# Four graph layers on one core: one-hots by place in the block, and sums joined on VectorE

## The chip, the cores and the metric

The kernel runs on one core of a Trainium2 chip. The metric is the device time in microseconds (us). Over three runs the median is 5306.94 us (5293.82 to 5309.91). One further execution was taken with the hardware profiler, and every line of profile in this document comes from such an execution.

## The reference

There are 6250 nodes with 256 features, and 100000 directed edges, sorted by their destination `dst`. Four layers of message passing follow each other. Each takes the normalised, rectified features, passes messages along the edges, sums them at the destination, and adds the result to `x`:

```python
h = jnp.maximum(_layernorm(x), 0.0); x = x + layer(h, ...)      # four times

# layer 0: attention with 8 heads, logits from per-node scores s, self loops
alpha = leaky_relu(s[src] + s[dst], 0.2)
e = exp(alpha - segment_max(alpha, dst)[dst])
attn = segment_sum(Vh[src] * (e / segment_sum(e, dst)[dst])[:, :, None], dst)
h = batch_norm(x + attn @ Wo + bo); h = batch_norm(h + relu(h @ W1 + b1) @ W2 + b2)
# layer 1: messages times a filter made from 32 edge features and a cutoff
agg = segment_sum(hl[src] * (rbf @ W_r2m.T + b_r2m) * C[:, None], dst)
# layer 2: attention with one head, logits from the gathered row and 128 edge features
out = relu(segment_sum(xj * softmax_by_dst(a)[..., None], dst))
# layer 3: graph convolution with self loops
out = relu(segment_sum(xw[src] * (dinv[src] * dinv[dst])[:, None], dst) + b)
```

Everything is fp32. What matters here is `segment_sum`: sums of edge rows, by destination, once in every layer (256 to 265 columns, 128 in layer 1).

## The kernel before, in words

The nodes are padded to 6272 and lie in 49 blocks of 128, node n on partition n mod 128. The edges lie in 98 groups of 1024, each as 128 partitions by 8 columns. As the edges are sorted, the destinations of group g fall into a window of 128 nodes that starts at node 64g − 32 (checked at run time; a slower path exists for other data and isn't taken here). `rel` holds each edge's destination relative to its window.

A stage of edges is a loop over the groups. For a group, GpSimd issues eight indirect DMAs (`gather`, L130), each of which fetches 128 source rows from a table in DRAM; they go into a ring of tiles, several groups ahead. VectorE makes eight one-hots of 128x128 (`rel` compared with `iota`, in layers 1 and 2 also multiplied by a weight). TensorE multiplies one-hots and rows in eight matmuls that add up in one PSUM tile S, two in turn (`sum_window`, L666 to L673; the eight matmuls are L670). In fp32 a matmul leaves two records in the trace. So S holds the sums of the window's nodes, with the window's first node on partition 0.

A window starts at partition 96 or 32 of a block, so the sums lie 32 or 96 partitions off. In layers 0, 2 and 3 ScalarE therefore copies S to SBUF (`ws`, L672; in layer 3 L1158), and `sum_block` (L675 to L681) builds block b's sum in a PSUM tile T out of up to four windows, each multiplied by a shifted identity (`shifts`, four matmuls at L680, on every second group). `blocks_done` tells after which group a block is whole.

The stages, in the order of the program, by the span of the profile:

- Rows of layer 0 (0 to 180 us): per block layernorm, transposes, the value row and the score terms, written to table `vt`. Between the blocks the list `checks` is worked off on VectorE, one entry after every fourth block; it fills `rel` too.
- e0 (180 to about 1430 us): layer 0's edges. `scw` holds the nodes' score terms laid out by window (four tiles made by shift matmuls at L706 to L712, copied at L714), and `place`, from GpSimd's iota at L716, the node number at each partition of a window. For group g: `logits0` (L746 to L756) uses the gathered rows and the destination's terms, which `of_dst` (L743) fetches with a transposed one-hot from L729; L816 multiplies the rows with the exponentials; L670 sums. On odd groups `attn0` (L758 to L766) finishes a block, `turn0` (L772 to L774) transposes it, and one group later `project0` (L780) and `residual0` (L788, L790) multiply it with the output weights. At groups 6 and 8, `made` prepares weights of layers 1 and 2 on TensorE and VectorE through PSUM tag B.
- Feed-forward and batch norms of layer 0, and the table for layer 1 (1432 to about 1867 us).
- e1 (gathers from 1700 to 2915 us): layer 1 sums with swapped operands (L1008), so that nodes lie along the columns: `agg`, with a column for each node. VectorE adds the columns that the last window has already begun (64 at L1035), ScalarE copies the others (64 at L1036). L994 multiplies a finished block, L1026 makes layer 2's table row.
- e2 (3017 to 4132 us, finished at 4177): layer 2, with `one_hot2` (L1075, logits and weight on VectorE and ScalarE), `sum_window`, `sum_block`, `out2`, and the table row for layer 3.
- e3 (4177 to 5292 us, finished at 5321): layer 3, with `one_hot3` (L1130), the sum at L1154, the copy at L1158, `sum_block`, and `end3` (L1134 to L1141), which adds the node's own row from `rows3`, scales, adds the bias, rectifies and writes out.

The order inside e0 to e3 is written by hand (`manual_schedule`): each engine works its instructions in the order of the program, and only semaphores between engines delay them. GpSimd's queue holds the gathers and little else; SP's queue holds the loads and stores of rows. [...]

Of the kernel before, what the change touches and what calls it, by code (L numbers as in the profile page):

```python
# [35 lines left out]
def tile_gnn(ctx: ExitStack, tc: tile.TileContext, a: dict, out: bass.AP, N: int):  # L36

# [70 lines left out]
    shifts = const.tile([P, 3 * P], F32, name="shifts")  # L108
    nc.gpsimd.memset(shifts, 0.0)
    make_identity(nc, shifts[:, P:2 * P])  # L110
# [78 lines left out]
    with ExitStack() as l0:  # L189
# [52 lines left out]
        def row0(b):  # L242
# [3 lines left out]
            for k in range(2):  # L246
# [13 lines left out]

        rel3 = rel.rearrange("p (g j) -> p g j", j=J)
# [5 lines left out]
                  lambda: nc.vector.tensor_scalar(bad[:, 1:2], bad[:, 1:2], P - 1.0, None, OP.subtract)]  # L267
# [377 lines left out]
    def fast():  # L645
        wp = fctx.enter_context(tc.tile_pool(name="wl", bufs=1))
        psc = fctx.enter_context(ExitStack())
        ps = psc.enter_context(Psum("ps0", S=2, A=2, T=1, B=2, E=1))

        def one_hot(pool, g):  # L650

            oh = pool.tile([P, J, P], F32, name="oh")
            nc.vector.tensor_tensor(oh, iota[:, None, :].to_broadcast([P, J, P]),
                                    rel[:, g * J:(g + 1) * J][:, :, None].to_broadcast([P, J, P]),
                                    OP.is_equal)
            return oh

        def shift_by(s):

            return shifts[:, P - s:2 * P - s]  # L660

        def windows_of(b):

            return [(g, HW * g - OFF - P * b) for g in range(max(0, 2 * b - 1), min(G, 2 * b + 3))]

        def sum_window(pool, oh, rows, n):  # L666

            s = ps("S", [P, n])
            for j in range(J):
                nc.tensor.matmul(s, oh[:, j, :], rows[:, j, :], start=j == 0, stop=j == J - 1)  # L670
            ws = pool.tile([P, n], F32, name="ws", bufs=6)
            nc.scalar.activation(ws, s, AF.Copy)  # L672
            return ws  # L673

        def sum_block(sums, b, n):  # L675

            t = ps("T", [P, n])
            parts = windows_of(b)
            for i, (g, s) in enumerate(parts):
                nc.tensor.matmul(t, shift_by(s), sums[g], start=i == 0, stop=i == len(parts) - 1)  # L680
            return t  # L681
# [16 lines left out]
        with tc.tile_pool(name="e0", bufs=2) as ep:  # L698

            scw = ep.tile([P, NB, 2, 2 * H], F32, name="scw", bufs=1)  # L700
            for odd in range(2):
                for b0, b1 in ((0, 32), (32, NB)):
                    t = ps("AB"[odd], [P, b1 - b0, 2 * H])
                    if odd:
                        b2 = min(b1, NB - 1)
                        nc.tensor.matmul(t, shift_by(-OFF), sc[:, b0:b1, :], start=True, stop=False)  # L706
                        nc.tensor.matmul(t[:, 0:b2 - b0, :], shift_by(P - OFF), sc[:, b0 + 1:b2 + 1, :],
                                         start=False, stop=True)
                    else:
                        b2 = max(b0, 1)  # L710
                        nc.tensor.matmul(t, shift_by(OFF), sc[:, b0:b1, :], start=True, stop=False)
                        nc.tensor.matmul(t[:, b2 - b0:, :], shift_by(OFF - P), sc[:, b2 - 1:b1 - 1, :],  # L712
                                         start=False, stop=True)
                    nc.vector.tensor_copy(scw[:, b0:b1, odd, :], t)  # L714
            place = ep.tile([P, G], F32, name="place", bufs=1)
            nc.gpsimd.iota(place, pattern=[[HW, G]], base=-OFF, channel_multiplier=1,  # L716
                           allow_small_or_imprecise_dtypes=True)
            sums, drows, tos, dgs, ohs, vs, ms, mts = {}, {}, {}, {}, {}, {}, {}, {}
# [73 lines left out]
            with tc.manual_schedule():  # L792
# [5 lines left out]
                for g in range(G + 2):  # L798
# [11 lines left out]
                    summed = [(b, sum_block(sums, b, VR)) for b in blocks_done(g - 1)]  # L810
# [8 lines left out]
                    for b, s in summed:  # L819
                        attn0(b, s)  # L820
                    if g < G:
                        sums[g] = sum_window(ep, ohs[g], vg, VR)
                    for b, s in summed:
                        turn0(b)
# [106 lines left out]
        with tc.tile_pool(name="e1", bufs=2) as ep, Psum("ps1", S=2, A=3, B=1, C=1, K=1) as ps:  # L931
# [7 lines left out]
            agg = ep.tile([P, HW * (G - 1) + P], F32, name="agg", bufs=1)  # L939
# [38 lines left out]
            with tc.manual_schedule():  # L978
# [6 lines left out]
                for g in range(G + 2):  # L985
# [6 lines left out]
                    for b in blocks_done(g - 1):  # L992
                        t = ps("B", [P, D])
                        nc.tensor.matmul(t, agg[:, OFF + b * P:OFF + (b + 1) * P], w1["out"],  # L994
# [36 lines left out]
                    if g < G:  # L1031
                        old = HW if g else 0
                        c = HW * g
                        if old:
                            nc.vector.tensor_tensor(agg[:, c:c + old], agg[:, c:c + old], s[:, 0:old], OP.add)  # L1035
                        nc.scalar.activation(agg[:, c + old:c + P], s[:, old:P], AF.Copy)  # L1036
# [9 lines left out]
        with tc.tile_pool(name="e2", bufs=2) as ep:  # L1046
            vgs, sums, normed = {}, {}, {}
# [60 lines left out]
            with tc.manual_schedule():  # L1108
                for g in range(G + 2):
                    if ahead <= g < G:  # L1110
                        rows2(g)
                    summed = [(b, sum_block(sums, b, TR)) for b in blocks_done(g - 1)]
# [3 lines left out]
                    for b, s in summed:  # L1116
                        normed[b] = out2(b, s)
                    if g < G:
                        sums[g] = sum_window(ep, oh, vgs[g], TR)
# [384 lines left out]
```

## Time and profile before

| what | value |
|---|---|
| median of three runs | 5306.94 us |
| profiled execution | 5323.26 us |
| its span | 5321.5 us |
| mean granted clock of TensorE | 0.746 |
| busy: TensorE, VectorE, ScalarE, GpSimd | 3068.8, 2089.9, 609.6, 3036.3 us |
| moved by DMA | 536.81 MB, 101 GB/s |

The span is the time from the first to the last instruction of the profiled execution. Busy times are sums over the span; an engine that waits or only issues is not busy. The granted clock says how fast TensorE was allowed to run, 1 being full speed. An idle time is put down to the event that ended it: the name of an instruction on another engine, "issue" where nothing visible held the engine, and "remote" where the event could not be traced to an instruction. PEld is TensorE's loading of weights, which overlaps with its matmuls.

### The profile page before, as it was taken

Reading aid. Unit: us, or ns where it says so; the run is one execution under the profiler, and the core shown is the slowest. Engines: PE = TensorE matmul, PEld = TensorE weight load, DVE = VectorE, ACT = ScalarE, POOL = GpSimd, SP = SyncE. Lnnn points to the kernel's source line nnn. Section 1 sums busy time; section 2 is a strip of 40 time slices with the busy share of each in tenths; the row PEclk is TensorE's granted clock in tenths of the full one; section 3 lists DMA queues with packets and bytes.
Section 4 is the critical chain, followed back from the end, with each engine's and each line's share of the span. In section 5 each row is a group of like instructions: output and inputs, shape, how many; then the busy total and the mean of one; then the engine's idle time right before and its main releaser. Section 6 shows DMA issues by size and latency. Waiting matters only on the chain.

```text
span 5321.5 us, 42644 instructions
## 1 busy us (share of the span) xinstructions
PE 3068.8 (58%) x12132; PEld 2383.4 (45%) x12133; DVE 2089.9 (39%) x6391; ACT 609.6 (11%) x1559; POOL 3036.3 (57%) x3215
## 2 busy tenths in 40 slices
PE   7577777787896144444444545555555345554545
PEld 4366666666645133333333434444444333443334
DVE  5355555555525155555555623333333112221222
ACT  3100000000134000000000012222222100000000
POOL 0456666666203655656555266666666566666665
PEclk9777777777897567777777777777777677776777
DMA  2444444444301233333333233333333233333332
GB/s 96 124 127 139 137 141 139 139 138 136 110 0 56 60 95 100 98 103 102 97 96 103 74 96 99 97 98 100 100 99 97 76 93 99 97 97 97 98 97 84
DMA packets 258746, 536.81 MB, mean 101 GB/s; under 512 B 65096, under 2 KB 144966, under 8 KB 258502
## 3 DMA queue, kind: packets, MB, share of 16 engines
q0 software_dynamic: 137984, 364.28, 25.3%
q1 hardware_dynamic: 107750, 156.85, 9.2%
q10 hardware_dynamic: 12768, 12.85, 0.8%
q8 instruction: 103, 1.69, 0.1%
q14 instruction: 141, 1.16, 0.1%
HBM read 504.57 MB, written 29.15 MB: 100 GB/s over the span
## 4 chain that ended last, share of the span: by engine, by line
PE 35%; another core or an unknown queue 23%; issue 18%; DVE 8%; POOL 8%; ACT 5%; DMA 2%; ACTq 0%; DVEq 0%; SPq 0%; POOLq 0%
PE ps_S L670 13%; PE ps_S L1154 5%; POOL vg L130 5%; PE ps_A L743 3%; POOL big L130 3%; PE ps_T L680 3%; DVE oh L968 2%; PE ps_A L441 2%; PE ps_B L447 2%; PE ps_Q L245 1%; DVE big L1005 1%; PE ps_S L1008 1%; PE ps_B L780 1%; ACT L1072 1%
## 5 line engine op out<-in xcount | busy, mean ns | idle before, releaser
L130 POOL DMA_INDIRECT vg<-xt,src_i x1568 | 1488.6, 949 | 888.7 <-issue 543.1
L130 POOL DMA_INDIRECT big<-ht,src_i x784 | 740.4, 944 | 482.8 <-PE ps_S L1008 185.2
L130 POOL DMA_INDIRECT xbuf<-vt,src_i x784 | 764.5, 975 | 437.2 <-PE ps_S L670 191.3
L670 PE MATMUL ps_S<-vg,oh 128*128 128x258 f32 x1568 | 473.1, 467 | 435.4 <-DVE oh L1075 422.5
L680 PE MATMUL ps_T<-ws,shifts 128*128 128x265 f32 (+2 forms) x1164 | 342.4, 435 | 479.7 <-issue 319.6
L670 PEld LDWEIGHTS ps_S<-vg,oh 128*128 128x128 f32 x1568 | 371.7, 241 | 523.5 <-DVE oh L1075 436.8
L1154 PE MATMUL ps_S<-vg,oh 128*128 128x256 f32 x1568 | 431.8, 428 | 162.7 <-issue 129.3
L670 PE MATMUL ps_S<-xbuf,oh 128*128 128x265 f32 x1568 | 497.6, 480 | 20.2 <-issue 18.2
L680 PEld LDWEIGHTS ps_T<-ws,shifts 128*128 128x128 f32 x1164 | 243.0, 214 | 559.5 <-issue 397.5
L1075 DVE TENSOR_SCALAR oh<-iota,rel,ex 128x128 f32<-128x128 f32 x784 | 210.4, 359 | 662.8 <-ACT ex L1072 510.1
L1154 PEld LDWEIGHTS ps_S<-vg,oh 128*128 128x128 f32 x1568 | 342.8, 219 | 238.2 <-issue 177.1
L670 PEld LDWEIGHTS ps_S<-xbuf,oh 128*128 128x128 f32 x1568 | 371.3, 243 | 109.6 <-issue 24.8
L1130 DVE TENSOR_SCALAR oh<-iota,rel 128x128 f32<-128x128 f32 x784 | 163.1, 296 | 579.8 <-remote 413.1
L1008 PE MATMUL ps_S<-oh,big 128*128 128x128 f32 x1568 | 287.2, 357 | 172.2 <-issue 138.0
L1008 PEld LDWEIGHTS ps_S<-oh,big 128*128 128x128 f32 x1568 | 276.6, 268 | 196.8 <-issue 149.7
L994 PE MATMUL ps_B<-wout,agg 128*128 128x256 f32 x98 | 55.9, 671 | 535.0 <-DVE agg L1035 368.1
L816 DVE TENSOR_TENSOR xbuf<-xbuf,ps_E 128x2048 f32<-128x2048 f32 x98 | 223.8, 2283 | 320.6 <-issue 145.0
L743 PEld LDWEIGHTS ps_A<-scw,to 128*128 128x128 f32 x1568 | 248.7, 246 | 61.9 <-DVE to L729 45.8
L743 PE MATMUL ps_A<-scw,to 128*128 128x16 f32 x1568 | 243.8, 301 | 52.0 <-DVE to L729 48.6
L994 PEld LDWEIGHTS ps_B<-wout,agg 128*128 128x128 f32 x98 | 23.6, 299 | 553.4 <-issue 330.8
L672 ACT ACTIVATE ws<-ps_S 128x265 f32<-128x265 f32 (+1 forms) x196 | 76.3, 389 | 1702.0 <-PE ps_S L670 803.1
L960 PE MATMUL ps_A<-wr,rb 99*128 99x384 f32 (+1 forms) x588 | 207.7, 493 | 9.3 <-issue 9.3
(228 smaller groups left out, 3419.5 us busy)
## 6 DMA issues: line engine op xcount, KB each, us to landing
drow<-in_dst_row SPq DMA_DIRECT2D x98, 512.0 KB
ea<-in_edge_attr SPq DMA_DIRECT2D x98, 512.0 KB
vg<-xt,src_i POOLq DMA_INDIRECT x1568
xbuf<-vt,src_i POOLq DMA_INDIRECT x784
big<-ht,src_i POOLq DMA_INDIRECT x784
rb<-in_rbf SPq DMA_DIRECT2D x196, 49.5 KB
vt<-row SPq DMA_DIRECT2D x49, 132.5 KB
xt<-row SPq DMA_DIRECT2D x49, 129.0 KB
```

What stands on the lines that cost most here:

```text
L130: nc.gpsimd.indirect_dma_start(out=rows, out_offset=None, in_=table, in_offset=bass.IndirectOffsetOnAxis(ap=idx[:, j:j + 1], axis=0))
L441: nc.tensor.matmul(t[:, :n], w["w1"][:, k, m * P:(m + 1) * P], hn[:, k, :n], start=k == 0, stop=k == 1)
L447: nc.tensor.matmul(t[:, :n], w["w2"][:, m, o * P:(o + 1) * P], f[:, m, :n], start=m == 0, stop=m == 3)
L670: nc.tensor.matmul(s, oh[:, j, :], rows[:, j, :], start=j == 0, stop=j == J - 1)
L680: nc.tensor.matmul(t, shift_by(s), sums[g], start=i == 0, stop=i == len(parts) - 1)
L743: nc.tensor.matmul(dgs[g][:, j, :], tos[g][:, j * P:(j + 1) * P], scw[:, g // 2, g % 2, :], start=True, stop=True)
L816: nc.vector.tensor_tensor(vals, vals, ex[:, :, :, None].to_broadcast([P, J, H, HD]), OP.mult)
L960: nc.tensor.matmul(t, rbs[g][0:33 * n, g % 2, q, :], wr3[0:33 * n, 0:n, :], start=True, stop=True)
L1008: nc.tensor.matmul(s, hg[:, j, :], ohs[g][:, j, :], start=j == 0, stop=j == J - 1)
L1075: nc.vector.tensor_scalar(oh[:, j, :], iota, rel[:, g * J + j:g * J + j + 1], ex[:, j:j + 1], OP.is_equal, OP.mult)
L1130: nc.vector.tensor_scalar(oh[:, j, :], iota, rel[:, g * J + j:g * J + j + 1], None, OP.is_equal)
L1154: nc.tensor.matmul(s, oh[:, J - 1 - j, :], vg[:, J - 1 - j, :], start=j == 0, stop=j == J - 1)
```

## The change: what it does

`rel` becomes the destination's place in its block, `dst & 127`, so that a sum lies on its own node's partition from the start. A window covers four quarters of 32 partitions, of two blocks; the shift matmuls and their constant go. Instead, `join` adds quarters of the last group's copy (`ws`) and of this group's PSUM sum on VectorE, into a PSUM tile T: two adds of 32 partitions per group, in e0 and e2. ScalarE's copy of S stays there. In layer 3 there is no copy: `add3` adds the PSUM sum into `rows3` directly, in two or three parts, and `end3` starts from there, with the bias in a PSUM tile. In layer 1 `agg` loses its offset, so that the additions and copies of 64 columns fall into pieces of 32 and 64. `scw` and `place` are made by copies on ScalarE and VectorE. T gets two PSUM banks, and B one. In e0, `join` stands behind the multiplication of the rows and ahead of `attn0`; in e2, behind the one-hots and ahead of `out2`; in e3, `add3` stands behind the next group's one-hots.

```diff
+                  lambda: nc.vector.tensor_single_scalar(rel.bitcast(I32), dst_i, P - 1, op=OP.bitwise_and),
+                  lambda: nc.vector.tensor_copy(rel, rel.bitcast(I32))]
...
-        ps = psc.enter_context(Psum("ps0", S=2, A=2, T=1, B=2, E=1))
+        ps = psc.enter_context(Psum("ps0", S=2, A=2, T=2, B=1, E=1))
...
-        def sum_block(sums, b, n):
-
-            t = ps("T", [P, n])
-            parts = windows_of(b)
-            for i, (g, s) in enumerate(parts):
-                nc.tensor.matmul(t, shift_by(s), sums[g], start=i == 0, stop=i == len(parts) - 1)
-            return t
+        def join(g, blocks, s, ws, n):
+
+
+            b = g // 2
+            quarters = [(b, 1), (b, 2)] if g % 2 else [(b - 1, 3), (b, 0)]
+            if g == G - 1:
+                quarters.append((b, 3))
+            for c, q in quarters:
+                if c < 0:
+                    continue
+                if c not in blocks:
+                    blocks[c] = ps("T", [P, n])
+                r = slice(q * Q, (q + 1) * Q)
+                if g == 0 or (g == G - 1 and q == 3):
+                    nc.vector.tensor_copy(blocks[c][r, :], s[r, :])
+                else:
+                    nc.vector.tensor_tensor(blocks[c][r, :], ws[r, :], s[r, :], OP.add)
...
+            nc.scalar.activation(scw[:, :, 0, :], sc, AF.Copy)
+            nc.vector.tensor_copy(scw[:, :, 1, :], sc)
+            nc.scalar.activation(scw[L, 1:NB, 0, :], sc[L, 0:NB - 1, :], AF.Copy)
+            nc.vector.tensor_copy(scw[F, 0:NB - 1, 1, :], sc[F, 1:NB, :])
...
-            nc.gpsimd.iota(place, pattern=[[HW, G]], base=-OFF, channel_multiplier=1,
-                           allow_small_or_imprecise_dtypes=True)
+            nc.vector.tensor_copy(place, nodeid[:, :, None].to_broadcast([P, NB, 2]))
...
-                    summed = [(b, sum_block(sums, b, VR)) for b in blocks_done(g - 1)]
...
-                    for b, s in summed:
-                        attn0(b, s)
+                    if 0 < g <= G:
+                        join(g - 1, totals, sums[g - 1], kepts.get(g - 2), VR)
+                    for b in blocks_done(g - 1):
+                        attn0(b, totals[b])
                     if g < G:
-                        sums[g] = sum_window(ep, ohs[g], vg, VR)
+                        sums[g] = sum_window(ohs[g], vg, VR)
+                        kepts[g] = kept(ep, sums[g], VR)
...
-                        if old:
-                            nc.vector.tensor_tensor(agg[:, c:c + old], agg[:, c:c + old], s[:, 0:old], OP.add)
-                        nc.scalar.activation(agg[:, c + old:c + P], s[:, old:P], AF.Copy)
+                        c = g // 2 * P
+                        if g == 0:
+                            old, new = [], [(0, 3 * Q)]
+                        elif g % 2 == 0:
+                            old, new = [(c - Q, c), (c, c + Q)], [(c + Q, c + 3 * Q)]
+                        else:
+                            old, new = [(c + Q, c + 3 * Q)], [(c + 3 * Q, c + P), (c + P, c + P + Q)]
...
+            def add3(g, s):
+                b = g // 2
+                parts = [(b, Q, 2 * Q), (b, 2 * Q, P), (b + 1, 0, Q)] if g % 2 else [(b - 1, 3 * Q, P), (b, 0, 3 * Q)]
+                for c, r0, r1 in parts:
+                    if 0 <= c < NB:
+                        nc.vector.tensor_tensor(rows3[r0:r1, c, :], rows3[r0:r1, c, :], s[r0:r1, :], OP.add)
+
+            def end3(b):
                 r0, r1 = b * P, min(N, (b + 1) * P)
-                nc.vector.tensor_tensor(s, s, rows3[:, b, :], OP.add)
-                nc.vector.scalar_tensor_tensor(s, s, dinv[:, b:b + 1], brow, op0=OP.mult, op1=OP.add)
+                t = ps("T", [P, D])
+                nc.vector.scalar_tensor_tensor(t, rows3[:, b, :], dinv[:, b:b + 1], bias, op0=OP.mult, op1=OP.add)
...
-                    sums[g] = ep.tile([P, D], F32, name="ws", bufs=6)
-                    nc.scalar.activation(sums[g], s, AF.Copy)
-                for b, s in summed:
-                    end3(b, s)
+                    sums[g] = s
+                if g > 0:
+                    add3(g - 1, sums[g - 1])
+                for b in blocks_done(g - 1):
+                    end3(b)
```

## The prediction

> **What bounds the kernel now.** I began with the slices of the page: TensorE, VectorE and GpSimd are all 40 to 60% busy, so nothing is full. The costliest groups come next (form, count | busy, mean ns | idle time before, and what ended it):
>
> ```profile
> L130 POOL DMA_INDIRECT vg<-xt,src_i x1568 | 1488.6, 949 | 888.7 <-issue 543.1
> ...
> L680 PE MATMUL ps_T<-ws,shifts 128*128 128x265 f32 (+2 forms) x1164 | 342.4, 435 | 479.7 <-issue 319.6
> ...
> L1154 PE MATMUL ps_S<-vg,oh 128*128 128x256 f32 x1568 | 431.8, 428 | 162.7 <-issue 129.3
> ```
>
> The shift matmuls that go away (L680) hold TensorE for 342 us. What they are worth depends on what each stage waits for, so the busy time by stage is next (columns: stretch, length, then busy time and count of PE, PE's weight loads, VectorE, ScalarE, GpSimd, then granted clock, DMA share, GB/s). The four rows are the edge stages of layers 0 to 3, called e0 to e3:
>
> ```profile
> 180.00:1379.00 1199.00, 878.04 (x3845) 735.74 (x3844) 603.47 (x1654) 88.63 (x327) 763.81 (x785) 0.76 0.48 140
> ...
> 1700.00:2915.00 1215.00, 520.22 (x2248) 412.65 (x2249) 585.96 (x1466) 51.59 (x211) 739.23 (x783) 0.69 0.35 96
> 3017.00:4132.00 1115.00, 588.59 (x2145) 471.19 (x2145) 333.75 (x1369) 235.95 (x461) 742.18 (x783) 0.73 0.36 98
> ...
> 4177.00:5292.00 1115.00, 542.95 (x1882) 422.53 (x1883) 214.03 (x882) 34.89 (x93) 743.91 (x783) 0.71 0.34 98
> ```
>
> e2 and e3 do different work and take the same 1115 us for the same 784 gathers: 1115/784 = 1.42 us per gather. The timeline of GpSimd in both shows how:
>
> ```profile
> 3405.21 0.94 POOL L130 DMA_INDIRECT vg<-xt,src_i  x1 [3.07 <-remote]
> 3406.46 0.95 POOL L130 DMA_INDIRECT vg<-xt,src_i  x1 [0.30 <-issue]
> ...
> 3427.99 0.95 POOL L130 DMA_INDIRECT vg<-xt,src_i  x1 [3.08 <-remote]
> ...
> 4576.28 0.94 POOL L130 DMA_INDIRECT vg<-xt,src_i  x1 [5.38 <-remote]
> ...
> 4622.18 0.94 POOL L130 DMA_INDIRECT vg<-xt,src_i  x1 [5.97 <-remote]
> ```
>
> Gathers issue 1.25 us apart, then pause until something "remote". e2 does 16 per 22.78 us (3405.21 to 3427.99), e3 32 per 45.90 us: 1.42 and 1.43 us per gather, though the rounds differ twofold. I read this as a service behind the gathers of 1.42 us each, with GpSimd running ahead of it. While it has a backlog the other engines learn of finished matmuls late; that is what the longest waits show:
>
> ```profile
> ACT ws L672 <- remote: 742.7, 77, 32.5
> ACT ws L1158 <- remote: 623.4, 31, 35.3
> ...
> DVE oh L1130 <- remote: 413.1, 30, 34.0
> ...
> DVE m L761 <- PE ps_S L670: 71.7, 12, 7.7
> ```
>
> (total us, times, longest.) Waits of 35 us for a copy of a sum long computed are not TensorE's doing. So e2 and e3 are bound by gathers. e0's 784 gathers at the same 1.42 would take 1115 of its 1199 us: 84 us in which the service lies idle, all that e0 can give back. e1 (narrower rows) goes by pairs of groups of some 25 us.
>
> **The change, part by part.** Sums are made against the profiled execution, 5323.3 us (span 5321.5 and 1.8 around it). It lies 16.3 above the median of the runs shown, 5306.9, and that difference is taken off at the end. A measurement of this kernel can tell about 0.3%, 16 us.
>
> Node stage: two more passes over the 128x784 destinations, about 1 us each on VectorE by the row of its 128x1024 compare (0.75 us), while POOL and SP are busy there; cost 0 to 2, taken 1. The eight shift matmuls and four copies of the window scores become copies on ScalarE and VectorE: the copies showed 0.44 to 0.69 us each, beside TensorE's node work. The place table leaves GpSimd's queue, where it began at 220.59 behind the first gathers; L729 waited 10.8 us for it. Group 0's chain starts earlier, but the gathers ran meanwhile; only the stall of some 5 us that follows, when the ring of rows is full, comes back: −5 (0 to −10).
>
> e0, steady. Per pair of groups, TensorE loses four shift matmuls and VectorE gains four adds of 32 partitions. Here is one odd group in the timeline:
>
> ```profile
> 627.78 1.95 PE L680 MATMUL ps_T<-ws,shifts 128*128 128x265 f32 x8
> ...
> 630.15 2.28 DVE L816 TENSOR_TENSOR xbuf<-xbuf,ps_E 128x2048 f32<-128x2048 f32 x1
> ...
> 630.38 1.93 PE L743 MATMUL ps_A<-scw,to 128*128 128x16 f32 x16 [0.65 <-DVE to L729]
> 632.35 0.41 DVE L761 TENSOR_TENSOR m<-v,ps_T 128x256 f32<-128x256 f32 x1
> 632.53 5.39 PE L670 MATMUL ps_S<-xbuf,oh 128*128 128x265 f32 x16 [0.22 <-issue]
> ```
>
> The 1.95 us of L680 end at 629.7, before L743 has its one-hot (630.2), and L670 waits for L816's end (632.4): here the removal saves nothing. Elsewhere L680 waits for the copy ws and L743 is queued behind it. To place the 84 idle us I let every gather of the timeline take 1.42 us after its issue, one behind the other, and looked where that runs dry: about 24 lie before 363 us (start, and the preparation of layer 1's weights at group 6); the other 60 are 0.5 to 0.8 per pair and eight stalls of some 4.6 where an odd group's sum comes too late to be seen before the backlog. How many go I can't read off; bounds: 0 and −60 from idle time, against +60 if more pairs miss. I take half of the gain, −30.
>
> The adds: the row of a 128x256 add is 0.41 us, step 0.46; a lane works on as many elements when 32 lanes run, so 4 x 0.46 = 1.85 us per pair. They lie behind L816, ahead of L761 and of the next one-hots L735; the sum L670 waits for neither, and in steady state VectorE idles half the time (603 of 1199), which hides them. Where the cover is gone, in the drain after the last gather, a pair takes 14.45 us and is VectorE's: 1.85 x 2.5 pairs = +4.5. **A rule against the change**: the Trainium skill, "VectorE: DVE Perf Modes", § Two Vector instructions with no wait between them, says that an instruction which starts in another group of 32 partitions than the last is held until all earlier ones have finished. The rows show the overlap it would lose: L761 started 0.08 us before L816's end. Six held instructions a pair would be 0.5 us, 1.2 more in the drain and 24 over e0's 49 pairs if uncovered. By the row it is 4.5, by the rule 5.7; I keep 4.5.
>
> PSUM goes from T=1, B=2 to T=2, B=1: the two weight preparations (groups 6 and 8) ping-pong between TensorE and VectorE through B; +3.5 (0 to 7). The transposes of L772 and the projection L780 share the one B too, but lie a group apart.
>
> e1: the offset layout makes an even group two adds of 32 columns where there was one of 64. The 128x8 operation L763 takes 0.17 and a 128x64 0.21; a step of 0.15 on the path after the sum, 49 times, is +7.4; the third copy per pair is ScalarE's (52 of 1215 us busy), nothing; the drain adds 0.6. Sum +8.
>
> e2: 0 while the gathers bound it, hidden under 1.42 x 16 = 22.8 us a round against 16.1 that a pair takes unhindered in the drain; after the last gather the join (2 x 0.46) stands ahead of the output chain, +2. e3: a copy, shift matmuls and one add become adds straight into the kept rows. The sum's PSUM buffer is now freed by VectorE behind its one-hots (8 x 0.21), 2.6 us after the sum is seen, while TensorE still has about 4 us of the next sum: 0. At the end two shift groups (1.89 and 1.46) and their copies go, two pairs of adds come: −3.5.
>
> Sum: 1 − 5 − 30 + 4.5 + 3.5 + 8 + 2 − 3.5 = −19.5. 5323.3 − 19.5 − 16.3 = **5287 us**, 0.4% below the median.
>
> **Rivals.** *Gathers everywhere* (0.15): e0 keeps its idle time too, the removed matmuls lay beside it. Then +10.5 on the same sum, 5317; 5291 to 5323 covers it. For it: the odd group above. Against it: 72 us in which L761 waited for TensorE's sums.
>
> *Slower: more late sums in e0* (0.32). Place: odd groups. The group restarts at 628.0 and its sum ends at 637.9, about 10 us later, when finished matmuls begin to be seen late; so the pair sits on the edge. Without the 1.95 us of shift matmuls TensorE idles ahead of L743 and may run slower: L743 is 1.93 us here and 3.43 at half clock, and "TensorE: Matmul & The Clock Gate", § Part 1, says that an idle window of about 3.4 us takes the clock to half. The row bears it out: this stretch had 0.86 granted, and after ten nearly idle microseconds 0.52. A half-clock sum adds 1.5 us or more, and each miss 4.6. By the row's present misses (8 of 49) nothing changes; by the rule a miss in every second pair is 16 x 4.6 = +74, without the gain of 30: 5391; in every pair 41 x 4.6 = +189, 5506. It decides from about the fifteenth miss (half of the gain eaten, and the 10.5 more).
>
> *A large gain* (0.11): the pauses in e2 and e3 belong to TensorE's events, not to a service. Then fewer matmuls let gathers run at 1.25: 0.17 x 784 x 2 = −267, 5020; or e0 loses its 60 whole: 5257. Against the first: the same 1.42 in rounds of two lengths.
>
> **How the numbers follow.** Forecast 0.42, from 5250 to 5300 and nearly all of it faster by more than 16. With 0.10 of the large gain faster is 0.52; same is 0.16 (the rival of gathers and the forecast's edge), slower 0.32. For 8 in 10, the low end takes in most of e0's idle time and some of the hidden stalls, 5215, the high end the slower case with a miss in every second pair, 5390.
>
> **What would show it.** Right: no L680, some 196 joins in e0 and as many in e2, each near 0.4 us, e2 and e3 at 1115 ± 3 us from first to last gather, e0's gathers in about 1165, e1 longer by some 7. Wrong: e0 at 1199 or above with GpSimd's gaps at even groups (late sums), a granted clock below 0.70 in e0, or rounds in e2 and e3 other than 22.8 and 45.9 us: then the service was not what bounds them.

## The result

The changed kernel takes 5382.7 us (median of four runs, 5368.3 to 5411.6) beside 5308.4 for the kernel before: a ratio of 1.0146, 95% interval 1.0113 to 1.0179. It is slower. The forecast was 5287 and faster; the time lies inside the range, on the side of the rival "more late sums in e0".

One thing has to be said ahead of all comparisons: the same kernel before took about 5310 us in some batches of runs, 5253 in others and 4498 in the rest. Each run below is therefore set beside the runs of the kernel before that were made in turn with it on the same chip, and that time is named ("beside 5318").

The profiled execution of the changed kernel took 5382.1 us (span 5380.3) against 5323.3. Its busy time over the four edge stages, from first to last gather (columns as in the table by stage of before):

```profile
182.00:1400.00 1218.00, 783.14 (x3460) 663.42 (x3461) 684.70 (x1832) 89.27 (x329) 768.24 (x784) 0.74 0.47 137
1727.00:2984.00 1257.00, 523.17 (x2251) 413.54 (x2252) 589.74 (x1510) 54.24 (x254) 745.14 (x784) 0.69 0.33 92
3085.00:4193.00 1108.00, 518.91 (x1780) 396.51 (x1779) 416.50 (x1556) 236.10 (x461) 746.60 (x784) 0.72 0.37 99
4241.00:5350.00 1109.00, 445.38 (x1504) 359.40 (x1504) 288.42 (x1055) 0.00 (x0) 747.27 (x784) 0.69 0.34 98
```

TensorE lost 95 us of work in e0, 70 in e2 and 98 in e3, and VectorE gained 81, 83 and 74. The time does not follow these amounts. By the first and last gather of each stage, the span's 58.8 us are: e0 +18.8, the stretch from e0's last gather to e1's first +7.3, e1 **+40.4**, e2 −8.7, e3 −7.5, and 8.5 in the rest (1.6 before e0, 0.1 between e1 and e2, 4.1 between e2 and e3, 2.7 at the end). The joins cost what was expected (operation, count, minimum, median and maximum in ns):

```profile
L682 DVE TENSOR_TENSOR ps_T<-ws,ps_S x388: 419/435/455, 263.4 to 4230.2; 32x265 f32<-32x265 f32 x97, 32x258 f32<-32x258 f32 x97
```

In e1 the picture changed more than its work. In GpSimd's timeline before, a round of 16 gathers stops after twelve, goes on, and the next round starts 6.38 us after the sixteenth:

```profile
2394.26 0.94 POOL L130 DMA_INDIRECT big<-ht,src_i  x1 [3.71 <-PE ps_S L1008]
...
2408.05 0.95 POOL L130 DMA_INDIRECT big<-ht,src_i  x1 [0.31 <-issue]
2410.32 0.94 POOL L130 DMA_INDIRECT big<-ht,src_i  x1 [1.31 <-remote]
...
2414.06 0.94 POOL L130 DMA_INDIRECT big<-ht,src_i  x1 [0.30 <-issue]
2420.44 0.94 POOL L130 DMA_INDIRECT big<-ht,src_i  x1 [5.43 <-PE ps_S L1008]
```

After, all sixteen go out without a stop, and the next round starts 8.47 us after the last:

```profile
2421.83 0.95 POOL L128 DMA_INDIRECT big<-ht,src_i  x1 [7.55 <-PE ps_S L1008]
...
2440.68 0.95 POOL L128 DMA_INDIRECT big<-ht,src_i  x1 [0.30 <-issue]
2449.15 0.95 POOL L128 DMA_INDIRECT big<-ht,src_i  x1 [7.53 <-PE ps_S L1008]
```

What the round waits for is the chain that begins with the table row's add on VectorE (the add in the round before, then the chain after):

```profile
2415.80 0.43 DVE L1026 TENSOR_TENSOR row<-ps_C,bn 128x258 f32<-128x258 f32 x1 [11.82 <-remote]
```

```profile
2444.54 0.43 DVE L1026 TENSOR_TENSOR row<-ps_C,bn 128x258 f32<-128x258 f32 x1 [13.20 <-remote]
2444.89 2.13 DVE L968 TENSOR_SCALAR oh<-iota,rel,cut 128x128 f32<-128x128 f32 x8
2446.94 0.28 DVE L1041 TENSOR_TENSOR agg<-agg,ps_S 128x32 f32<-128x32 f32 x2
2447.13 1.34 DVE L1005 TENSOR_TENSOR big<-big,ps_A 128x384 f32<-128x384 f32 x3
```

From L1026 to the gathers' restart it is 4.61 us here and 4.64 before (2415.80 to 2420.44): the extra piece of 32 columns costs nothing visible. But L1026 itself is released later. If each gather takes 1.42 us from its issue, one behind the other, these sixteen are worked off at 2444.55, and L1026 starts at 2444.54. Before, they were worked off at 2416.98 and L1026 started 1.18 us ahead of that. This pair of rounds is a clear case and not the typical one: over the 49 rounds L1026 starts at the median 1.3 us ahead before and 0.7 us ahead after. By the same reckoning the service idles 105 us in all of e1 before and 145 after, which is e1's whole growth.

### The profile page after: what moved, and what is told of

Its sections match the earlier page's. It is cut to its first block, busy times and chain, and to the rows that moved or that the text cites. A ratio compares the mean times of both kernels' runs of the same rounds, so it can differ in the third digit from the quotient of the medians.

```text
span 5380.3 us, 40826 instructions
## 1 busy us (share of the span) xinstructions
PE 2802.3 (52%) x10952; PEld 2166.3 (40%) x10953; DVE 2351.2 (44%) x7031; ACT 577.2 (11%) x1511; POOL 3050.5 (57%) x3211
## 4 chain that ended last, share of the span: by engine, by line
another core or an unknown queue 26%; PE 19%; DVE 13%; issue 7%; ACT 4%; POOL 2%; DMA 0%; DVEq 0%; ACTq 0%; POOLq 0%
PE ps_S L1174 8%; PE ps_S L655 5%; DVE oh L968 3%; DVE big L1005 2%; DVE oh L1084 2%; DVE ea L1010 2%; DVE te L1011 2%; PE ps_A L442 2%; PE ps_B L448 2%; POOL big L128 1%; POOL vg L128 1%; ACT L1081 1%; ACT L124 1%; PE ps_S L1008 1%
## 5 line engine op out<-in xcount | busy, mean ns | idle before, releaser
L1174 PE MATMUL ps_S<-vg,oh 128*128 128x256 f32 x1568 | 461.3, 465 | 674.7 <-issue 598.3
L1174 PEld LDWEIGHTS ps_S<-vg,oh 128*128 128x128 f32 x1568 | 372.7, 242 | 763.6 <-issue 659.4
L655 PEld LDWEIGHTS ps_S<-vg,oh 128*128 128x128 f32 x1568 | 368.6, 241 | 606.9 <-DVE oh L1084 489.8
L1026 DVE TENSOR_TENSOR row<-ps_C,bn 128x258 f32<-128x258 f32 x49 | 20.9, 427 | 497.3 <-remote 468.7
L968 DVE TENSOR_SCALAR oh<-iota,rel,cut 128x128 f32<-128x128 f32 x784 | 209.4, 349 | 0.0
```

Of the source, the lines that this page charges most:

```text
L968: nc.vector.tensor_scalar(ohs[g][:, j, :], iota, rel[:, c], w1["cut"][:, c], OP.is_equal, OP.mult)
L1174: nc.tensor.matmul(s, oh[:, J - 1 - j, :], vg[:, J - 1 - j, :], start=j == 0, stop=j == J - 1)
```

## Experiments

### The parts alone

The changed kernel's e0 in the kernel before (four small operations ahead of layer 1 turn `rel` back from places in the block to places in the window):

```diff
 # e0, row stage, scw, place and PSUM shares of the changed kernel; layers 1 to 3 of the kernel before
+        turn_rel(False)      # rel = rel - start + 128 * (rel < start), start 96 or 32
```

> The changed kernel's e0 alone (with its row stage, scw, place, joins, PSUM shares), and the kernel before in layers 1, 2 and 3; between them four small VectorE operations turn the places in the block back into places in the window, some 2 us. Theory E0, that the loss on the slower chips lies in e0 (joins and the single B bank, more late sums): on a chip where the kernel before takes 5250 to 5310, +30 to +75 us; on one where it takes 4498, within 8 us. Rival E1, that the loss lies in layer 1's pieces of 32 columns: within 20 us of before on either.

Measured: 5361.1 us beside 5318.1, ratio 1.0112 (1.0065 to 1.0160).

The changed kernel's layer 1 in the kernel before:

```diff
+        turn_rel(True)
 # e1 of the changed kernel: agg without offset, pieces of 32 and 64 columns
+        turn_rel(False)
```

> The kernel before with the changed kernel's layer 1 alone (agg without offset, pieces of 32 and 64 columns), and eight small VectorE operations around it that turn the places, some 4 us. The split of the add alone did not lengthen e1 on a slower chip (1168 against 1216), so theory E0 says: within 20 us of before on a slower chip, within 8 on a faster one. Rival E1: +25 to +45 on a slower chip.

Measured: 5344.3 beside 5318.1, ratio 1.0050 (1.0033 to 1.0067). And the whole, beside both:

> The changed kernel as a whole on the same chip as the two parts. On a slower chip +50 to +90 us over the kernel before, as in the first result, on a faster one within 5. If the parts add up, this is new_e0 plus new_e1 plus what layers 2 and 3 give; by theory E0 nearly all of it is new_e0's.

Measured: 5379.6, ratio 1.0153 (1.0089 to 1.0217). So the loss repeats, and within the intervals its parts add up: 1.12% and 0.50% make 1.62. Both theories were half right: by these medians e0 has some two thirds and layer 1 the other third. By the first profile it is the other way round (+18.8 and +40.4), so the split is known only roughly. In layer 1 the longer stage comes with the new code, by the stage rows of new_e1 and then of new_e0, whose layer 1 is the old one:

```profile
1689.00:2940.00 1251.00, 516.97 (x2252) 410.25 (x2253) 588.92 (x1507) 54.24 (x254) 743.74 (x784) 0.69 0.34 93
```

```profile
1702.00:2898.00 1196.00, 527.58 (x2254) 414.64 (x2255) 591.78 (x1468) 52.65 (x211) 742.86 (x784) 0.69 0.35 97
```

In these batches e1's gathers took 1256, 1248 and 1250 us with the new code (the changed kernel twice, new_e1) and 1216 and 1194 with the old.

For e0 I laid the service of 1.42 us per gather against every profile, as in the prediction, and counted where it runs dry. "Long stalls" are those of 2.9 us or more after group 8:

| profile | e0's code | beside | e0's gathers, us | groups 0–5, idle us | groups 6–8 | long stalls | their sum |
|---|---|---|---|---|---|---|---|
| before | old | 5308 | 1198 | 8.1 | 17.0 | 8 | 37.0 |
| new_e1 | old | 5318 | 1190 | 6.5 | 17.0 | 7 | 26.7 |
| after | new | 5308 | 1217 | 1.1 | 28.7 | 12 | 54.4 |
| after_third | new | 5318 | 1213 | 1.6 | 21.9 | 11 | 54.0 |
| new_e0 | new | 5318 | 1192 | 1.7 | 22.6 | 6 | 28.6 |
| load_before | old | 5253 | 1155 | 6.6 | 10.6 | 1 | 3.0 |
| load_after | new | 5253 | 1208 | 0.6 | 21.7 | 13 | 61.3 |

(The loads of the last two lie in layers 1 to 3 only.) Three of the four profiles with the new e0 have more stalls than any with the old. The fourth, new_e0, has no more than the old code: it is the shortest of its four runs, 5305 of 5305 to 5405. With the new code stalls come in trains (in new_e0 too, at groups 70, 72, 74 and 84, 86, 88): after has them at groups 58, 60, 62, 64, 66, 68, 70 and 72; before has them at 12, 32, 44, 52, 62, 70, 78 and 86. This is a stall that repeats, in the changed kernel (the gathers restart; the odd sum; the next eight gathers; the copy of that sum):

```profile
995.50 1.29 POOL L128 DMA_INDIRECT xbuf<-vt,src_i  x1 [6.10 <-PE ps_S L655]
...
1003.30 3.82 PE L655 MATMUL ps_S<-xbuf,oh 128*128 128x265 f32 x16 [1.28 <-issue]
...
1005.88 0.97 POOL L128 DMA_INDIRECT xbuf<-vt,src_i  x1 [0.30 <-PE ps_S L655]
...
1015.62 0.39 ACT L661 ACTIVATE ws<-ps_S 128x265 f32<-128x265 f32 x1 [14.56 <-remote]
```

The sum is complete at 1007.1 and seen at 1015.6, while eight more gathers went out behind its first matmuls. The trace's records of TensorE's own signals show the delay: from 1004.19 on they stand at 1005.61, 1007.04 and 1008.46, 1.42 us apart like the gathers of the service, and the one that lets the copy go at 1015.60. In the kernel before, the odd sum after a stall (restart at 655.80) began at 664.1; its first matmul was not seen before the eight gathers were worked off. Then eight signals of TensorE stand within 0.30 us (667.31 to 667.61), and the whole sum is seen at 667.93:

```profile
664.07 3.83 PE L670 MATMUL ps_S<-xbuf,oh 128*128 128x265 f32 x16
...
664.55 0.94 POOL L130 DMA_INDIRECT xbuf<-vt,src_i  x1 [0.30 <-issue]
667.61 1.29 POOL L130 DMA_INDIRECT xbuf<-vt,src_i  x1 [2.12 <-PE ps_S L670]
...
667.93 0.39 ACT L672 ACTIVATE ws<-ps_S 128x265 f32<-128x265 f32 x1 [6.47 <-PE ps_S L670]
```

### Which piece does it

The next kernels take one piece each.

Fewer shift matmuls in the kernel before (only the first window of each block is summed; the others are left out). With it, for layer 1, ScalarE's copy in two parts:

```diff
-            parts = windows_of(b)
+            parts = windows_of(b)[:1]
...
-                        nc.scalar.activation(agg[:, c + old:c + P], s[:, old:P], AF.Copy)
+                        n = 32 if g % 2 else P - old
+                        for k in range(old, P, n):
+                            nc.scalar.activation(agg[:, c + k:c + k + n], s[:, k:k + n], AF.Copy)
```

> The same kernel as in the run before, for another chip: one shift matmul per block in e0, e2 and e3, and the copy of odd groups in e1 in two parts. On a slower chip, theory P: e0's stalls in trains, 45 us or more together; rival Q: 37 or less. Theory S: e1 1235 to 1260; its rival: within 15 of 1200. On a faster chip as before.

Measured: 5250.0 beside 5253.9, ratio 1.0001 (0.9974 to 1.0027). No long stall at all in e0, and e1's gathers in 1162 us:

```profile
181.00:1329.00 1148.00, 833.60 (x3584) 692.59 (x3585) 605.53 (x1662) 88.79 (x327) 771.03 (x785) 0.76 0.50 146
1644.00:2807.00 1163.00, 531.82 (x2252) 413.46 (x2253) 595.67 (x1468) 56.63 (x254) 742.81 (x784) 0.68 0.36 100
```

Theory P expected trains, and in this profile fewer shift matmuls did not start one. That is not the end of P: no stall came that could have repeated, and the profile is the shortest of 19 runs, 5192 to 5262 (the ratio over all of them shows no loss). Theory S found no support either, but beside 5253 even the whole new layer 1 did not lengthen e1 in the one pair of profiles there (the loads below), so half of it can't decide. The same edits also ran beside 4498, apart and together:

> The kernel before with only the first of up to four shift matmuls of each block (layers 0, 2 and 3 leave the other windows' sums out of a block); nothing is put in their place. Theory A, that the shift matmuls lie beside the gathers: e2 and e3 stay within 10 us of 1115 each, e0 within 15 of 1199, total -0.6 to 0%. Rival B, that they are on the path in e0: e0 -30 or more with fewer than 4 long stalls. Rival C, that TensorE's events end the gathers' pauses: e2 and e3 fall by 30 us or more each. Rival D, that less work on TensorE lowers the clock: granted clock in e0 below 0.72 and e0 longer by 15 or more.

> The kernel before with only the first of up to four shift matmuls of each block (layers 0, 2 and 3 leave the other windows' sums out), as before on a faster chip. In the profiles of the slower chips the old e0 has 1 to 8 long stalls, one at a time (27 to 37 us in two profiles), the new e0 11 to 13, in trains at every second group (54 to 61 us). Theory P: after a stall the old kernel's odd sum starts 8.3 us behind the gathers' restart, its first matmuls aren't seen before the backlog of 8 gathers is worked off, and then all are seen at once; without the 1.5 to 2 us of shift matmuls it starts 7.8 behind, its first matmuls are seen, eight more gathers go out on them, and the rest is held back for another 11 us: the stall repeats. Then this kernel on a slower chip has trains: stalls of 45 us or more in all, e0 +10 to +30 against before, total +0.2 to +0.6%. Rival Q, that the joins on VectorE and the single B bank make the stalls: stalls as before or fewer, total -0.5 to 0%. On a faster chip nothing, as before.

> The kernel before, with only this: in e1 ScalarE's copy of 64 columns (L1036) is made in two of 32 on odd groups, as in the changed kernel; VectorE's add stays whole. On slower chips e1 took 1248 to 1256 with the changed kernel's layer 1 and 1194 to 1216 with the old one; the split of the add alone had 1168 on another. Theory S, that ScalarE's third copy delays the next block's transposed rows (L1017) and with them the row's sum: e1 1235 to 1260, total +0.4 to +0.7%. Rival, that neither piece alone does it: e1 within 15 of 1200, total within 0.25%.

Measured: one_shift 0.9994 (0.9985 to 1.0003), one_shift_slow 0.9999 (0.9991 to 1.0008), e1_copies 1.0000 (0.9992 to 1.0009), and shift_copies, both edits, 1.0000 (0.9991 to 1.0008). e2 stayed at 986 and e3 at 982: the shift matmuls cost nothing there.

Adds like the joins in the kernel before, in addition to the shift matmuls (they read two kept sums in SBUF, where a join reads one in PSUM, and nobody waits for them), and layer 1's add of 64 columns in two; first apart, then in one kernel:

```diff
+                    if 1 < g <= G:
+                        for q in ((1, 2) if g % 2 == 0 else (3, 0)):
+                            r = slice(32 * q, 32 * q + 32)
+                            nc.vector.tensor_tensor(extra[r, :], sums[g - 2][r, :], sums[g - 1][r, :], OP.add)
...
-                        if old:
-                            nc.vector.tensor_tensor(agg[:, c:c + old], agg[:, c:c + old], s[:, 0:old], OP.add)
+                        n = old if g % 2 else old // 2
+                        for k in range(0, old, n or 1):
+                            nc.vector.tensor_tensor(agg[:, c + k:c + k + n], agg[:, c + k:c + k + n],
+                                                    s[:, k:k + n], OP.add)
```

> The kernel before, with four more VectorE adds of 32 partitions by 265 per pair of groups in e0, at the place where the changed kernel joins; they add two kept sums into a scratch tile that nobody reads; shift matmuls stay. Theory A, that VectorE's idle time hides them until the drain: e0's gathers within 10 us of 1199, drain +4 to +6. Rival B, that they push pairs over the edge so that more odd sums come too late: e0 +15 to +60 with 12 to 20 long stalls in place of 8. e1 to e3 within 5 us in either case.

> The kernel before, with only this: in e1 the add of 64 columns (L1035) of every even group is split into two of 32, so that VectorE has one more operation per pair of groups, 0.07 to 0.15 us longer. Theory A, that a small delay of the odd group's sum costs a whole step of the gathers' service of 0.7 to 1.4 us per pair: e1's gathers take 25 to 45 us longer (1215 becomes 1240 to 1260), the total rises by as much (+0.5 to +0.8%), all other stages within 5 us. Rival B, that the operation costs what it lasts: +5 to +7 us in e1, total within 0.3%. Rival C, that ScalarE's extra copies or the layout without offset made e1 longer in the changed kernel: 0 to +7 here.

> The kernel before with both of the earlier single edits: four unread adds per pair in e0, and the add of 64 columns of even groups in e1 in two parts. Where gathers go every 1.25 us: e0 +10 to +14, e1 within 2 of 980, as in the two runs above. Where they take 1.42 us with pauses: theory A says e1 +25 to +45 and e0 +15 to +60; rival B says e1 +7 and e0 0.

Measured beside 4498: e0_adds 1.0028 (1.0017 to 1.0040), with e0's gathers in 1032 us where the other variants of the old e0 took 1017 to 1022; e1_split 1.0001 (0.9993 to 1.0010). Beside 5253: adds_split 1.0028 (0.9978 to 1.0079), four long stalls of 17.3 us together, e1 1168. So the adds cost some 12 us where gathers go out every 1.25, and beside 5253 no train came with them, though e0's gathers took 1177 us where load_before, on the same chip, took 1155. The add in two parts costs nothing beside 4498; beside 5253 the interval is as wide as the loss of layer 1 that it should explain. Against theory A of layer 1, a step of the service for every 0.1 us, speaks that in adds_split the odd sum starts the same 0.1 us later behind the restart (6.44 us for 6.33) as in the changed kernel, and e1 is not long.

PSUM's shares, alone, and then with both of layer 1's pieces:

```diff
-        ps = psc.enter_context(Psum("ps0", S=2, A=2, T=1, B=2, E=1))
+        ps = psc.enter_context(Psum("ps0", S=2, A=2, T=2, B=1, E=1))
```

> The kernel before, with only PSUM's share in e0 changed to that of the changed kernel (T=2, B=1). Theory A, that the two weight preparations at groups 6 and 8 and little else suffer: the gap of the gathers at groups 6 and 8 grows by some 12 us, e0 by 10 to 15, total +0.2 to +0.3%. Rival B, that the single B bank also delays transposes and projections of the later groups: more late odd sums (8 long stalls become 12 or more), e0 +25 to +40. Rival C, nothing: within 5 us.

> The kernel before with edits in two stages: in e0 PSUM's shares of the changed kernel (T=2, B=1); in e1 both the add of even groups and the copy of odd groups in two parts of 32 columns, with the layout unchanged. Alone, neither the missing shift matmuls nor the four adds made stalls come in trains in e0, and neither half of e1's pieces made e1 longer. In the slower state: if the B bank makes the trains, e0's stalls are 45 us or more together and 22 or more at groups 6 to 8 (17 or 9 before); if the two pieces of e1 together pay what neither pays alone, e1 is 1235 or more. If neither, stalls 37 or less and e1 below 1215, and the cause is in what was not tried alone: joins that attn0 waits for, and the layout of layer 1. In the faster state total within 0.1% of before.

Measured: 0.9997 (0.9989 to 1.0006) and 0.9998 (0.9990 to 1.0007), both beside 4498. Neither has been seen beside 5250 or 5310, so the question they were made for stays open.

Matmuls in the place of the removed ones, in the changed kernel:

```diff
+                e = ps("E", [P, 512])
+                exs[g] = e[:, 0:J * H].rearrange("p (j h) -> p j h", h=H)
+                for _ in range(4 * (g % 2)):
+                    nc.tensor.matmul(e[:, 256:512], ident, kepts[g - 1][:, 0:256], start=True, stop=True)
```

> The changed kernel with, in e0, four matmuls of 128x256 per odd group where the shift matmuls had stood, from the identity and the last kept sum into unused columns of PSUM's E bank, which nobody reads. Theory P: stalls come singly again (35 us or less), e0 -15 to -30 against the changed kernel, total +0.7 to +1.2% over before on a slower chip. Rival Q: stalls in trains as in the changed kernel, total +1.4% or more. On a faster chip within 5 us of the changed kernel.

Measured: 0.9993 (0.9984 to 1.0002) beside 4498.7. It tells nothing of the trains.

### Where the gathers aren't held back

> The changed kernel itself, beside the kernel before on the same chip. In the four runs above the kernel before took 4498 us, not 5307, and its gathers went out every 1.25 us nearly without pause in e1, e2 and e3; the service of 1.42 us behind the gathers is not a constant of the kernel. Theory A, that the loss comes from late sums and service steps: where gathers take 1.25 us, e1, e2 and e3 stay within 3 us of 980, 985 and 982 and only e0 is longer, by about 12 (the adds alone gave +11.6 in e0), with +2 at the group 6 and 8 preparations and +8 in the drains: total +0.3 to +0.6%; where they take 1.42 us, the first result again, +1.5%, with e1 +40 and e0 +19. Rival B, that the loss is work on the path in e1 whatever the gathers do: e1 +40 here too.

Measured: 4496.6 beside 4497.7, ratio 0.9998 (0.9989 to 1.0007): no loss and no gain. The stages of the changed kernel there:

```profile
181.00:1200.00 1019.00, 776.03 (x3627) 649.25 (x3628) 711.52 (x1917) 100.63 (x343) 779.30 (x784) 0.82 0.58 169
1492.00:2472.00 980.00, 645.47 (x2524) 481.72 (x2524) 669.04 (x1695) 61.08 (x286) 741.39 (x784) 0.76 0.46 125
2492.00:3477.00 985.00, 549.41 (x1834) 419.48 (x1835) 435.10 (x1597) 249.53 (x475) 743.03 (x784) 0.77 0.42 112
3498.00:4481.00 983.00, 566.56 (x1552) 434.88 (x1552) 303.31 (x1105) 0.00 (x0) 742.96 (x783) 0.73 0.39 111
```

784 gathers at 1.25 us are 980: GpSimd's issuing bounds three stages, and kernels with the old code have the same three lengths beside 4498 (e0_one_b: 980, 986 and 982). The 12 us more that were expected in e0 did not come: its gathers took 1017 us, as with the old code. Rival B, 40 us of work on the path in e1 whatever the gathers do, is out: the work is the same and e1 is not longer.

The order of layer 1, with the one-hots of the next group ahead of L1026:

```diff
+                    if g + 1 < G:
+                        one_hot1(g + 1)
                     for b, r in rows:
                         row = ep.tile([P, TR], F32, name="row2")
...
-                    if g + 1 < G:
-                        one_hot1(g + 1)
```

> The kernel before, with only this: in e1 the eight one-hots of the next group (L968) stand ahead of the table row's add (L1026) on VectorE, instead of behind it, so that 2.1 us of one-hots no longer lie between the row's late sum and the next group. Theory A: where the gathers' service takes 1.42 us and idles 2.7 us per pair of groups, e1 falls by 1.5 to 2.1 us per pair, 70 to 100 us (1215 becomes 1115 to 1145), total -1.3 to -1.9%; where gathers go every 1.25 us, nothing (e1 980). Rival B, that the service's steps only shift: e1 within 15 us on either.

Measured: 4499.8 beside 4497.7, 1.0003 (0.9994 to 1.0012), e1 983. Where it was meant to help it has not run.

Are the held-back events a matter of how many there are? Small loads on SP's queue:

```diff
+        def more_events(n):
+            for _ in range(n):
+                k = nx[0] % 16
+                nx[0] += 1
+                nc.sync.dma_start(extra_i[:, 16 * k:16 * k + 16], a["src"][0:16, 16 * k:16 * k + 16])
```

> The kernel before, with small extra loads on SP's queue into a scratch tile that nobody reads (16 rows of 64 bytes each): 8 per group of edges in e1, 4 in e2, 16 in e3. Each leaves semaphore events of its own, as each gather does; the data is small. Theory E, that in the first profile the pauses came from semaphore events being served one after the other, and not from data: with enough extra events the same picture appears on a chip without it: pauses of the gathers, sums seen late, e3 above 1050 and e1 above 1020 us. Rival F, that the first chip was slow for a reason that events do not touch: e1, e2 and e3 stay within 15 us of 980, 985 and 982. If the chip is one where the kernel before takes 5300: e1 and e3 longer by 100 or more by theory E.

> The changed kernel with the same extra loads. By theory E, with pauses in e1: e1 is longer than in the kernel before with the same loads by 20 to 40 us. By rival F: the same stage times as in the kernel before with the loads, within 5 us.

Measured: load_before 5275.5 beside 5252.5, ratio 1.0145 (1.0104 to 1.0186); load_after 5391.7 (two runs), 1.0267 (1.0174 to 1.0360). Sixteen more loads per group left e3's gathers at 1112.8 us and eight left e1's at 1203.5, within what the old code had without them. Theory E fell for such loads: they add events, and the stages don't get longer. The kernel as a whole pays at its end, where the loads queue ahead of the stores (54 us after the last gather, 29 before). With the same loads the changed kernel is slower by 116 us; of the 96 between the two profiles 52 lie in e0, 2 in e1, 11 in e2 and 24 at the end. So here, beside 5253 and with the loads, the new layer 1 costs 2 us and not 40, although its odd sums start 6.43 us behind the restart as in the first profile: the new code alone does not make e1 long. Whether the batch or the loads took the loss away, no run tells.

## Why the prediction was wrong

Of the 78 us between the forecast sum (−19.5) and the profiled span (+58.8), e0 has 50 and e1 32; the rest makes −4.

- **"e0, steady: I take half of the gain, −30."** This step failed. The long stalls rose from 37.0 us to 54.4, and to 54.0 in a second profile: +17, where −30 stood. It priced the service's idle time as work that is queued and shrinks when work leaves the path. As far as the traces show it, the stalls go by whether a sum is seen before or behind a backlog, and an edit can move that either way. The bounds took in +60; the value was taken from the wrong side. The prediction's own sign of being wrong came: e0 at 1217 us, with the pauses at even groups.
- **"e1: +8."** This step failed too. The step of 0.15 us on the path 49 times was the wrong model: L1026 to the restart is as long as before, 4.6 us. In the clear rounds L1026 is released later, and e1 grew by 40; layer 1 alone in the old kernel costs 0.50%, 26 us. Why, stays open: the halves of its pieces ran only beside 4498 and 5253, where the whole did not lengthen e1 either (beside 5253 in the pair with the loads).
- **The single B bank, +3.5 (0 to 7).** Groups 6 to 8 idle 28.7 and 21.9 us with the new e0, 17.0 with the old: +12 and +5 (beside 5253, 21.7 for 10.6). That it is the bank is argued from the place, not shown.
- **The start of e0, −5.** Right: 8.1 and 6.5 us of idle service became 1.1 and 1.6.
- **The drains.** +4.5 and +0.6 forecast; the stretch from e0's last gather to e1's first grew by 7.3. After e2 it was 4.1 where 2 stood, and after e3 2.7 more where 3.5 less stood; but in the second profile these two stretches were 4.8 and 3.7 us shorter than before. The values aren't steady enough to tell.
- **e2 and e3, 0.** Near right: −8.7 and −7.5 in the first profile, 1128.5 and 1112.9 us in the second. That 98 us less on TensorE buys next to nothing in e3 (7.5 and 2.3 us) held in every batch.
- **The rule on held instructions.** The joins' median is 0.435 us, and L682 starts two in 0.91 us: a step of 0.46 to 0.48. The row was right, the rule changes little here.
- **The rival that came in** named the place, late odd sums in e0, and the edge. Its price, 4.6 us per miss, was right (54.4/12 = 4.5); its cause, a colder TensorE, has little behind it: e0's granted clock went from 0.76 to 0.74. It had not seen that misses come in trains. That 5383 lies beside its 5391 is luck: it stood for a miss in every second pair and +8 in e1, and there were 12 misses and +40.

What stays open: which part of the new e0 starts the trains. Beside 5253, fewer shift matmuls alone had no long stall and the adds alone four, where the old e0 had one and the new one 13. The joins that `attn0` waits for, the single B bank there, and the parts together were not taken apart; nor is it known what makes the new layer 1 long beside 5310 and not in the pair beside 5253.

## What to carry to other kernels

When engines wait long for work that was long done ("remote"), the busy times don't price an edit, in either direction: look at when each sum is complete against the backlog that holds it, and don't settle on faster or slower unless that order is known. Put each stage of a many-stage change alone into the old kernel: here that split a loss of 1.5% into 1.1 and 0.5 at once, where single pieces told little. And put a piece where the whole is known to cost: where the whole costs nothing, a half of it can tell nothing. Before a wait is taken for a property of the kernel, see whether it is there in another batch of runs.

## What was not expected of the hardware

- The same program ran in 4498, 5253 and 5310 us. It is not the chip alone: one chip gave 4497.7 for the kernel before in one batch and 5253.9 in another. In the first kind gathers leave every 1.25 us nearly without pause; in the others they take 1.40 to 1.44 on average in e2 and e3, with either kernel.
- In the longer ones it isn't the data that is late. In the stretch from 4600 to 4640 us of before, in 40 slices of 1 us, the DMA engines are less than a tenth busy in slices 19, 22 and 23 while ScalarE and VectorE wait for sums; after that the gathers restart at 4622.18:

```profile
DMA  3325422344233442230210012443644432344332
```

  The whole trace holds 23,013 records of semaphore changes (the signals between engines) there and 73,233 in the changed kernel beside 4498, of the gathers' landings 9,815 and 50,191. So "remote" in the longer runs can also be an event whose record is missing. Of TensorE's signals, 1097 come within 0.05 us of the one ahead of them in the profile of the kernel before, and 632 in the first of the changed kernel, as if let go together; in the eleven profiles beside 4498 not one does. What holds the events back, no run here shows.
- An engine's longer pause can follow from an earlier event: in e0's trains, first matmuls seen early let eight gathers go ahead of the rest of the same sum, whose signals then come about 1.42 us apart, and which is seen 8.5 us late (1007.1 to 1015.6).
